# Expert tiles of two sizes: pairs of 128-slot units, and single units for an odd rest

## Chip, core and metric

The kernel runs on one core of one Trainium2 chip. The metric is the device time of that core in microseconds. Before the change it is 7677.54 us, the median of three runs (7675.36 to 7677.76).

## What is computed

The input is x, float32, 4 images of 256 channels by 64 x 64 pixels.

```
x = x + conv3(layernorm_over_channels(x))
t = tokens(x)                      # 4 x 4096 tokens of 256
z = layernorm(t)
probs = softmax(z @ gate_w + gate_b)          # 8 experts
for the two largest probs e of each token:
    t += probs[e] * (gelu(z @ W1[e] + b1[e]) @ W2[e] + b2[e])   # 256 -> 512 -> 256
x = pixels(t)
```

conv3 is three modulated deformable 3 x 3 convolutions in a row, each followed by relu. For every pixel and each of nine taps an offset and a mask are computed by an ordinary 3 x 3 convolution; the input is sampled bilinearly at the shifted place, scaled by the mask and multiplied by that tap's 256 x 256 weight. All of it is float32.

## The kernel before

**Convolutions.** An image is eight blocks of 512 pixels. A block of a layer is nine taps. For each tap and each 128 pixels, GpSimd gathers 128 rows of four corner vectors, 512 KB, from a table in HBM (`samples`, L503); VectorE combines them (L509, L514), ScalarE scales (L517), TensorE transposes (L532), ScalarE copies out of PSUM (L535), and TensorE multiplies with the tap's weight (`finish`, L555). That is four gathers a tap, 864 taps in the kernel, one after the other in the order of `self.stages`; the convolutions of one image and parts of the next alternate. `off_block` (L357 to L427) makes the offsets of a coming block.

**Experts.** When the last layer of a block is done, `tokens` makes its tokens, their normalised form and their two experts with weights. Tokens are taken in five groups: images 0, 1 and 2 whole (M = 32 columns of 128 tokens), image 3 in two halves (M = 16). When a group is complete, `route` (L690) gives each of its 2 x 128 x M token-expert pairs a slot, sorted by expert. An expert's slots begin at a multiple of 256 (FT), so that every tile of 256 slots belongs to one expert. A group has NF = 2 x M x 128 / 256 + 7 tiles, room enough whatever the routing: 39 for a whole image, 23 for a half; 163 in all, or 326 units of 128 slots. Tiles past the last used slot are worked like the others. `invert` (L768) turns slots into the list `tok` of the token in each slot by matmuls of one-hot matrices, and `wrow` holds the rows of the weight table for each tile. Where a tile's expert is that of the tile before in its chain, `wrow` points out of bounds and nothing is read.

A tile is worked by the generator `expert` (L825) in three pieces:
- `fetch` (L790), called at the end of the tile before, issues on GpSimd's queue the weights w (L800, 1.18 MB, two buffers in turn) and the token rows zt (L812, two gathers of 128 rows)
- piece 1: the y of the tile before is added and stored (`products`, L883: L892 and a store on SP's queue), four transposes (L840), one copy (L844)
- piece 2: 8 float32 matmuls of 256 columns, which stand in the trace as 16 records, two for each (L856), and four gelus (L866)
- piece 3: the next tile's fetch, then 8 matmuls of 256 columns, again 16 records (L874), into py

When all tiles of a group are done, `end` fetches each token's two results (L915), adds them with their weights (L930), transposes (L948) and stores.

**Order.** Tiles are taken from two chains in turn, f = 0, half, 1, half + 1, ... (`Group.order`), so that consecutive tiles use the two weight buffers. Pieces wait in three lanes (`Lane`): routes, tiles and sums. `pump` gives each lane one tap's credit after each tap of the convolution, and a lane runs pieces while its credit lasts. A tile costs `pace` taps: 5, 6, 2, 1.5 and 0 for the five groups. What is left after the last tap is drained: group 3 in part, group 4 entirely. `issue_after` keeps some instructions behind the newest gather, sum or transpose. A scheduler orders the instructions within these limits; each engine then works in its own order.

Of the kernel before, what the change touches and what calls it, by code (L numbers as in the profile page):

```python
# [8 lines left out]
F32 = mybir.dt.float32  # L9
# [73 lines left out]
class Group:  # L83


    def __init__(self, b, n0, n1):
# [4 lines left out]
        self.NF = 2 * self.M * P // FT + E - 1  # L91


        self.half = (self.NF + 1) // 2
        self.zt, self.acc, self.gy, self.sums, self.py = {}, [], [], [], None
        self.order = [s // 2 + s % 2 * self.half for s in range(self.NF)]

# [20 lines left out]
class Weave:  # L118
# [92 lines left out]
    def ffn_constants(self):  # L211
# [8 lines left out]
        nf = max(g.NF for g in self.groups)  # L220
        for g in self.groups:
            g.zd = self.dram.tile([g.M * P, C], F32, name=f"z_{g.nm}", tag=f"z_{g.nm}")
        self.ys = [
            self.dram.tile([nf * FT, C], F32, name=f"ys_{i}", tag=f"ys_{i}") for i in range(3)
# [42 lines left out]
        assert FU * nf <= P  # L267
# [422 lines left out]
    def route(self, grp):  # L690
# [3 lines left out]
        grp.tok = self.rt2.tile([P, FU * NF], I32, tag="tok", name=f"tok_{grp.nm}")  # L694
        grp.wrow = self.rt2.tile([P, NF], I32, tag="wrow", name=f"wrow_{grp.nm}")

        def small(tag, shape, dt=F32):
# [18 lines left out]
        nc.vector.tensor_scalar(ni, slot[:, :, M - 1], float(FT - 1), None, ALU.add)  # L716
        nc.vector.tensor_scalar(ni, ni, FT_LOG, None, ALU.logical_shift_right)
        nt = small("nt", (P, E))
        nc.vector.tensor_copy(nt, ni)
        end = small("end", (P, E))  # L720
        nc.vector.tensor_tensor_scan(end, self.ones[:, :E], nt, 0.0, ALU.mult, ALU.add)
        off = small("off", (P, E))
        nc.vector.tensor_tensor(off, end, nt, ALU.subtract)
        nc.vector.tensor_scalar(off, off, float(FT), None, ALU.mult)
        nc.vector.tensor_tensor(slot, slot, tot, ALU.subtract)
        nc.vector.tensor_tensor(slot, slot, rp[:, 0], ALU.add)
        nc.vector.tensor_tensor(
            slot, slot, off.unsqueeze(2).to_broadcast([P, E, M]), ALU.add
        )
        for i in range(2):  # L730
# [8 lines left out]
        past = small("r1", (P, NF, E))  # L739
        nc.vector.tensor_tensor(  # L740
            past,
            self.row_f[:, :NF].unsqueeze(2).to_broadcast([P, NF, E]),
            end.unsqueeze(1).to_broadcast([P, NF, E]),
            ALU.is_ge,
        )
        ex = small("ex", (P, NF))
        nc.vector.tensor_reduce(ex, past, AX.X, ALU.add)
# [18 lines left out]
        grp.inv = self.ps1.tile([P, FU * NF], F32, tag="py", name=f"inv_{grp.nm}")  # L766

    def invert(self, grp, m):  # L768
# [4 lines left out]
        n = FU * grp.NF  # L773
# [16 lines left out]
    def fetch(self, grp, step):  # L790
# [18 lines left out]
        for u in range(FU):  # L809
            zt = self.ffn.tile([P, C], F32, tag=f"zt{u}", name=f"zt_{grp.nm}_{f}_{u}")  # L810
            j = FU * f + u
# [13 lines left out]
    def expert(self, grp, step):  # L825
# [10 lines left out]
        zt = grp.zt.pop(step)  # L836
        tp = self.ps.tile([P, CC, FT], F32, tag="tp", name=f"ftp_{nm}")
        for u in range(FU):
            for c in range(CC):
                nc.tensor.transpose(  # L840
                    tp[:, c, u * P : (u + 1) * P], zt[u][:, c * P : (c + 1) * P], self.ident
                )
# [301 lines left out]
```

## Time and profile before

| | |
|---|---|
| median of three runs | 7677.54 us |
| the profiled execution | 6731.9 us, span 6730.2 us |
| granted TensorE clock in it | 0.979 |
| TensorE / VectorE / ScalarE / GpSimd busy | 92 / 74 / 49 / 66% of the span |
| bytes moved | 2228 MB, mean 331 GB/s |
| L503, gathers of the taps | 3456, 1059 ns each on GpSimd, 6.9 us to landing |
| L555, tap matmuls | 6912 records, 3404 us busy |
| L856, first expert matmul | 2608 records of 256 columns, 686 us busy |
| L874, second expert matmul | 2608 records of 256 columns, 659 us busy |
| L892, y | 163, 684 ns each |
| L800, weight fetches | 163 issued, 1112 ns each on GpSimd |
| L812, token gathers | 326, 1016 ns each on GpSimd |

The profiled execution is shorter than the runs of the median. Times below that come from the profile are those of this execution. PE is TensorE, PEld its weight loads, DVE VectorE, ACT ScalarE, POOL GpSimd, SP the sync engine that issues direct transfers. "L503" is line 503 of the kernel printed above. A group of instructions with one line is named by output and input tile, as in ph<-fzT,w. "Busy" of TensorE contains the pipelined ends of its matmuls, so the distance from one start to the next tells more than the duration of a record.

### The profile page before, as it was taken

The page shows a single profiled execution, that of the slowest core. Times are in us where ns is not written, and L with a number is a line of the kernel's source. Part 1 is how long each engine was busy: PE and PEld are TensorE (multiplying, and loading weights), DVE is VectorE, ACT ScalarE, POOL GpSimd, SP SyncE. Part 2 cuts the span into 40 slices and gives each one's busy share as a digit, 9 for nine tenths or more (in the row PEclk, how much of TensorE's full clock was granted, in tenths as well). Part 3 has the DMA queues.
Part 4 walks back from the last instruction along what each step waited for, and adds up shares of the span by engine and source line. Part 5 has one row for each costly group of instructions (what it writes and reads, how often), then busy time and mean ns, then how long its engine had stood idle before and what let it go on. Part 6 is the DMA issues. An engine that isn't in the chain of part 4 may idle for free. (4 is left out here: it accounts for less than half of the span.)

```text
span 6730.2 us, 88993 instructions
## 1 busy us (share of the span) xinstructions
PE 6193.9 (92%) x26500; PEld 3512.7 (52%) x26500; DVE 4955.9 (74%) x11467; ACT 3271.0 (49%) x7139; POOL 4463.9 (66%) x4245
## 2 busy tenths in 40 slices
PE   7999889899999999999999999999998999988987
PEld 3444344444555555555554555555554566655665
DVE  7878777899966767888977777667888764688511
ACT  3555555555544544555544554455554444444322
POOL 4656666666766666666777766666667775677643
PEclk9999999999999999999999999999999999999998
DMA  8999999999989989999899999989999997899744
GB/s 303 350 335 382 364 355 372 376 382 385 352 319 363 333 300 373 345 358 364 312 363 356 380 337 343 332 315 359 351 362 330 340 315 261 296 346 335 236 138 125
DMA packets 805215, 2228.45 MB, mean 331 GB/s; under 512 B 105016, under 2 KB 307768, under 8 KB 798976
## 3 DMA queue, kind: packets, MB, share of 16 engines
q0 software_dynamic: 551200, 1947.35, 78.3%
q1 hardware_dynamic: 253536, 275.41, 11.9%
q8 instruction: 215, 3.52, 0.2%
q14 instruction: 264, 2.16, 0.1%
HBM read 2165.40 MB, written 196.40 MB: 351 GB/s over the span
## 5 line engine op out<-in xcount | busy, mean ns | idle before, releaser
L503 POOL DMA_INDIRECT g<-tab,idx x3456 | 3660.1, 1059 | 1728.6 <-DVE s L514 602.0
L555 PE MATMUL acc<-sT,wk 128*128 128x512 f32 x6912 | 3404.2, 605 | 147.9 <-ACT sT L535 132.7
L509 DVE SCALAR_TENSOR_TENSOR g<-g,cf 128x512 f32<-128x512 f32 x3456 | 2558.2, 743 | 337.0 <-DMA g<-tab,idx 332.9
L514 DVE SCALAR_TENSOR_TENSOR s<-g,cf 128x256 f32<-128x256 f32 x3456 | 1658.4, 482 | 718.2 <-PE tp L532 438.3
L535 ACT COPY sT<-tp 128x512 f32<-128x512 f32 x1728 | 1001.5, 585 | 1852.9 <-PE tp L532 1850.3
L517 ACT ACTIVATE s<-s,cf 128x256 f32<-128x256 f32 x3456 | 1639.5, 508 | 360.0 <-DVE s L514 323.6
L555 PEld LDWEIGHTS acc<-sT,wk 128*128 128x128 f32 x6912 | 1161.3, 192 | 944.1 <-issue 641.3
L532 PEld LDWEIGHTS tp<-ident,s 128*128 128x128 f32 x6912 | 887.1, 143 | 1354.7 <-issue 661.7
L532 PE MATMUL tp<-ident,s 128*128 128x128 f32 x6912 | 1254.1, 280 | 185.6 <-ACT s L517 173.5
L856 PE MATMUL ph<-fzT,w 128*128 128x256 f32 x2608 | 686.3, 395 | 56.5 <-ACT fzT L844 31.9
L874 PE MATMUL py<-w,hT 128*128 128x256 f32 x2608 | 658.5, 387 | 28.8 <-ACT hT L866 25.4
L856 PEld LDWEIGHTS ph<-fzT,w 128*128 128x128 f32 x2608 | 479.9, 195 | 196.1 <-ACT fzT L844 67.7
L874 PEld LDWEIGHTS py<-w,hT 128*128 128x128 f32 x2608 | 469.1, 191 | 152.0 <-ACT hT L866 68.4
L866 ACT ACTIVATE hT<-ph,w 128x256 f32<-128x256 f32 x652 | 281.9, 471 | 462.3 <-PE ph L856 443.0
L812 POOL DMA_INDIRECT zt<-z,tok x326 | 331.3, 1016 | 152.0 <-issue 85.4
L357 PE MATMUL po<-win,wo 128*32 128x504 f32 (+1 forms) x2304 | 349.7, 597 | 1.0 <-ACT win L301 0.5
L915 POOL DMA_INDIRECT gy<-ys,slots x256 | 267.5, 1045 | 118.2 <-issue 73.2
L800 POOL DMA_INDIRECT w<-in_W,wrow x163 | 181.3, 1112 | 248.0 <-issue 122.3
L892 DVE TENSOR_TENSOR y<-py,w 128x512 f32<-128x512 f32 x163 | 111.5, 684 | 232.8 <-PE py L874 232.7
L930 DVE SCALAR_TENSOR_TENSOR ta<-gy,cw,ta 128x256 f32<-128x256 f32 x256 | 120.8, 480 | 109.3 <-DMA gy<-ys,slots 59.1
L357 PE MATMUL po<-win_pre,wo 128*32 128x504 f32 (+1 forms) x1152 | 187.1, 630 | 2.3 <-ACT om L366 2.0
L844 ACT COPY fzT<-ftp 128x512 f32<-128x512 f32 x163 | 95.4, 585 | 138.6 <-PE ftp L840 132.8
(154 smaller groups left out, 2902.5 us busy)
## 6 DMA issues: line engine op xcount, KB each, us to landing
tab<-hv SPq DMA_DIRECT2D x512, 128.0 KB
g<-tab,idx POOLq DMA_INDIRECT x3456, 6.9
ys<-y SPq DMA_DIRECT2D x163, 256.0 KB
tab<-h_pre SPq DMA_DIRECT2D x128, 256.0 KB
wk<-in_conv_w SPq DMA_DIRECT2D x117, 256.0 KB
xc_pre<-in_x SPq DMA_DIRECT2D x32, 512.0 KB
xr_tok<-in_x SPq DMA_DIRECT2D x32, 512.0 KB
t<-t_tok SPq DMA_DIRECT2D x32, 512.0 KB
```

What stands on the lines that cost most here:

```text
L357: nc.tensor.matmul(po[g * Q : (g + 1) * Q, :].rearrange("q (r w) -> q r w", w=W)[:, :, x0:x1], lhsT=self.wo[l][:, 3 * ky + kx, c, :], rhs= ...
L503: self.gathered = nc.gpsimd.indirect_dma_start(out=g.rearrange("p x s f -> p (x s f)"), out_offset=None, in_=self.table(*self.stages[i][:2 ...
L509: nc.vector.scalar_tensor_tensor(g[:, :, 0, :], g[:, :, 1, :], cf[:, j, 0:1], g[:, :, 0, :], ALU.mult, ALU.add,)
L514: self.last = nc.vector.scalar_tensor_tensor(s, g[:, 1, 0, :], cf[:, j, 1:2], g[:, 0, 0, :], ALU.mult, ALU.add)
L517: nc.scalar.activation(s, s, AF.Copy, scale=cf[:, j, 2:3])
L532: self.turned = nc.tensor.transpose(tp[:, c, u * P : (u + 1) * P], ss[u][:, c * P : (c + 1) * P], self.ident)
L535: nc.scalar.copy(self.sT[:, :, t0 * P : (t0 + 2) * P], tp)
L555: nc.tensor.matmul(acc[:, o, :], lhsT=self.wk[k][:, c, o * P : (o + 1) * P], rhs=sT[:, c, :], start=(k == 0 and c == 0), stop=(k == K - 1 ...
L812: self.nc.gpsimd.indirect_dma_start(out=zt, out_offset=None, in_=grp.zd, in_offset=bass.IndirectOffsetOnAxis(ap=grp.tok[:, j : j + 1], axi ...
L856: nc.tensor.matmul(ph[:, h, :], lhsT=w1[:, o : o + P], rhs=zT[:, c, :], start=(c == 0), stop=(c == CC - 1),)
L866: nc.scalar.activation(ht[:, h, :], ph[:, h, :], AF.Gelu, bias=w1[:, k : k + 1])
L874: nc.tensor.matmul(py[:, u, :], lhsT=hT[h // 2][:, h % 2, u * P : (u + 1) * P], rhs=w2[:, h * C : (h + 1) * C], start=(h == 0), stop=(h == ...
```

## The change

An expert with u units of 128 slots now gets u // 2 tiles of two units and, where u is odd, one tile of one unit. A group then needs at most 2 x M + 7 units: 71 in place of 78 for an image, 39 in place of 46 for a half. The first NP tiles (31 or 15) are pairs, the last nine are singles, 40 or 24 tiles in all. Pairs of all experts come first, in the order of experts, then the odd units in the order of experts; pairs beyond NP are worked as two singles.

`route` computes the slots from two running counts, one of pairs and one of odd units, and the expert of each tile likewise. A single transposes, multiplies, adds and stores half as much; its weight fetch is whole. The pace of a single is half that of a pair. `half` and the two chains are formed as before, from the new number of tiles.

```diff
-        self.NF = 2 * self.M * P // FT + E - 1
+        self.NU = 2 * self.M + E - 1
+        self.NP = (self.NU - E - 1) // FU
+        self.NF = self.NP + E + 1
...
+    def units(self, f):
+        return (FU * f, FU) if f < self.NP else (f + self.NP, 1)
...
-        nc.vector.tensor_scalar(ni, slot[:, :, M - 1], float(FT - 1), None, ALU.add)
-        nc.vector.tensor_scalar(ni, ni, FT_LOG, None, ALU.logical_shift_right)
+        nc.vector.tensor_scalar(ni, slot[:, :, M - 1], float(P - 1), None, ALU.add)
+        two = small("two", (P, 2, E), I32)
+        nc.vector.tensor_scalar(two[:, 0], ni, FT_LOG, None, ALU.logical_shift_right)
+        nc.vector.tensor_scalar(
+            two[:, 1], ni, FT_LOG - 1, 1, ALU.logical_shift_right, ALU.bitwise_and
+        )
...
+        over = small("r1", (P, E, M))
+        nc.vector.tensor_tensor(over, slot, cut.unsqueeze(2).to_broadcast(every), ALU.is_ge)
         nc.vector.tensor_tensor(
-            slot, slot, off.unsqueeze(2).to_broadcast([P, E, M]), ALU.add
+            over, over, off[:, 1].unsqueeze(2).to_broadcast(every), ALU.mult
+        )
+        nc.vector.tensor_tensor(slot, slot, over, ALU.add)
+        nc.vector.tensor_tensor(
+            slot, slot, off[:, 0].unsqueeze(2).to_broadcast(every), ALU.add
         )
...
+        for v in range(2):
+            past = small("r1", (P, NF, E))
+            nc.vector.tensor_tensor(
+                past,
+                first.unsqueeze(2).to_broadcast([P, NF, E]),
+                end[:, v].unsqueeze(1).to_broadcast([P, NF, E]),
+                ALU.is_ge,
+            )
+            nc.vector.tensor_reduce(part if v else ex, past, AX.X, ALU.add)
...
-        for u in range(FU):
+        q, fu = grp.units(f)
+        for u in range(fu):
             zt = self.ffn.tile([P, C], F32, tag=f"zt{u}", name=f"zt_{grp.nm}_{f}_{u}")
-            j = FU * f + u
+            j = q + u
...
-        nc.scalar.copy(zT, tp)
+        nc.scalar.copy(zT[:, :, :n], tp[:, :, :n])
...
                     nc.tensor.matmul(
-                        ph[:, h, :],
+                        ph[:, h, :n],
                         lhsT=w1[:, o : o + P],
-                        rhs=zT[:, c, :],
+                        rhs=zT[:, c, :n],
...
-                nc.scalar.activation(ht[:, h, :], ph[:, h, :], AF.Gelu, bias=w1[:, k : k + 1])
+                nc.scalar.activation(
+                    ht[:, h, :n], ph[:, h, :n], AF.Gelu, bias=w1[:, k : k + 1]
+                )
...
-        for u in range(FU):
+        for u in range(fu):
             for h in range(HC):
                 nc.tensor.matmul(
                     py[:, u, :],
...
-            self.ys[grp.i % 3][f * FT : (f + 1) * FT, :].rearrange("(u p) c -> p u c", u=FU),
-            y,
+            self.ys[grp.i % 3][q * P : (q + fu) * P, :].rearrange("(u p) c -> p u c", u=fu),
+            y[:, :fu],
...
             gen = self.expert(grp, step)
+            pace = grp.pace * grp.units(grp.order[step])[1] / FU
             for _ in range(3 + (step == 0)):
-                self.tiles.put(grp.pace / 3, lambda gen=gen: next(gen, None))
+                self.tiles.put(pace / 3, lambda gen=gen: next(gen, None))
```

## The prediction, made before the change was timed

> **What bounds the kernel now.** I read the page's first part, then the busy time of each engine in five stretches, then the tap gathers in the same stretches, then TensorE's timeline.
>
> ```profile
> PE 6193.9 (92%) x26500; PEld 3512.7 (52%) x26500; DVE 4955.9 (74%) x11467; ACT 3271.0 (49%) x7139; POOL 4463.9 (66%) x4245
> ...
> DMA packets 805215, 2228.45 MB, mean 331 GB/s; under 512 B 105016, under 2 KB 307768, under 8 KB 798976
> ...
> q8 instruction: 215, 3.52, 0.2%
> q14 instruction: 264, 2.16, 0.1%
> ```
>
> TensorE is far ahead of the other engines, but a busy share of pipelined matmuls overstates, so the stretches decide (columns: stretch, length, busy us of PE, PEld, DVE, ACT, POOL, granted clock, DMA share, GB/s). The first has no expert tiles, the next three have those of images 0, 1 and 2 beside the taps, the last is the drain.
>
> ```profile
> 672.00:1176.00 504.00, 448.56 (x1758) 204.96 (x1758) 390.34 (x772) 254.16 (x562) 338.07 (x322) 1.00 0.96 364
> 1848.00:3024.00 1176.00, 1119.29 (x4798) 637.62 (x4796) 864.53 (x1890) 603.10 (x1327) 772.36 (x746) 0.99 0.93 342
> 3528.00:4872.00 1344.00, 1251.55 (x5235) 692.75 (x5235) 987.52 (x2010) 678.31 (x1487) 931.74 (x890) 0.99 0.94 347
> 5208.00:5880.00 672.00, 654.77 (x2938) 422.91 (x2937) 421.51 (x859) 316.18 (x695) 448.74 (x440) 1.00 0.87 303
> 6384.00:6680.00 296.00, 265.34 (x1177) 214.08 (x1177) 46.74 (x110) 69.52 (x160) 108.92 (x112) 0.94 0.41 126
> ```
>
> Without tiles the DMA share is 0.96 and TensorE has 11% free; beside tiles TensorE is at 93 to 97% and the DMA share falls. So taps alone are bound by the gathers, taps with tiles by TensorE, with the DMA close behind; the drain by TensorE and its waits. How far each holds is read from the gathers of L503 (POOL's count) in the same stretches:
>
> ```profile
> 672.00:1176.00 504.00, 338.07 (x322) 1.00 0.96 364
> 1848.00:3024.00 1176.00, 670.06 (x649) 0.99 0.93 342
> 3528.00:4872.00 1344.00, 799.66 (x768) 0.99 0.94 347
> 5208.00:5880.00 672.00, 296.84 (x290) 1.00 0.87 303
> ```
>
> A gather takes 504/322 = 1.565 us without tiles. The 649 of image 0's stretch would then take 1016 us; the other 160 us fell to about 33 tiles (counted by the y adds of L892), 4.9 us a tile. The same sum gives 142/32 = 4.4 us for image 1 and 218/34 = 6.4 us for image 2. TensorE's own time for a tile follows from its timeline, start to start:
>
> ```profile
> 3000.86 1.04 PE L532 MATMUL tp<-ident,s 128*128 128x128 f32 x8
> 3001.96 1.99 PE L856 MATMUL ph<-fzT,w 128*128 128x256 f32 x8
> 3003.79 3.60 PE L555 MATMUL acc<-sT,wk 128*128 128x512 f32 x8
> 3007.22 3.62 PE L874 MATMUL py<-w,hT 128*128 128x256 f32 x16
> 3010.67 1.04 PE L532 MATMUL tp<-ident,s 128*128 128x128 f32 x8
> ```
>
> Sixteen py records take 3.45 us, 216 ns each; eight acc records of 512 columns 3.43 us, 429 ns each; transposes of 128 columns 110 ns. Time is by columns. A tile has 16 ph and 16 py records and 4 transposes: 3.45 + 3.45 + 0.44 = 7.35 us. So a tile costs the stretch 0.6 to 0.9 of its TensorE time, because the taps alone would have waited for gathers anyway. In the drain it costs more than that time:
>
> ```profile
> 6659.41 2.86 PE L874 MATMUL py<-w,hT 128*128 128x256 f32 x12 [0.19 <-ACT hT L866]
> ...
> 6667.61 2.86 PE L874 MATMUL py<-w,hT 128*128 128x256 f32 x12 [0.19 <-ACT hT L866]
> ```
>
> One tile each 8.20 us, with 0.56 and 0.19 us of waits for gelu, and longer waits where new weights come.
>
> [...] the 16 lp_tok matmuls of 8 columns took 1.71 us, 107 ns each[...]. [...] the weight fetch of 1.18 MB here landed in a median of 5.9 us:
>
> ```profile
> DMA to landing us min/median/max: 3.3/5.9/10.4
> ```
>
> **The change, part by part.** Each group loses 8 tiles of two units and gains 9 of one (39 to 31 + 9, in the halves 23 to 15 + 9).
>
> TensorE: a single has 16 ph records of 128 columns, 8 py records and 2 transposes. The ph record isn't in the trace: between 107 ns (load and stream overlapped) and 214 ns (one after the other). I take 110, as the transposes, which load a new operand each time too, run so; the other end is a rival. That makes 1.76 + 1.73 + 0.22 = 3.71 us. A group saves 8 x 7.35 - 9 x 3.71 = 25.4 us, or 3.46 tiles; the five save 127 us of TensorE. On the path: image 0 3.46 x 4.9 = 17, image 1 15, image 2 22, and the two halves of image 3, whose tiles lie mostly in the drain, 3.46 x 8.2 = 28 each. Sum 110 us.
>
> Weights: the expert of each tile follows from the routed pairs. Running the reference's router on its inputs gives 9 9 8 8 9 8 9 9 units in group 0 (the others alike: 3 to 5 odd experts a group), which makes 45 real fetches before and 13, 12, 12, 13, 12 = 62 after, as each odd expert's single needs its weights again. The page confirms the 45: packets of 8 KB or more are 805215 - 798976 = 6239, less 215 + 264 of instructions = 5760 = 45 x 128 rows. Bytes: 17 x 1.18 = +20 MB, less 35 units x 262 KB of zt and y = -9 MB. In images 0 to 2 that is 10 fetches less 21 units, +6.3 MB, 18 us at 345 GB/s; these stretches are bound by DMA for about 0.4 of a tile, so 7 us. Bounds 0 and 31 us.
>
> Weight waits: two buffers take turns, so a fetch starts when the tile before the current one has been added (L892) and has the current tile to hide behind. It takes 1.0 us of POOL and 5.9 of DMA, 6.9 us, against 8.2 us for a pair and some 4.1 us for a single. In the drain, pairs alternate with singles; the last group refetches for four pairs after a single, at 2.8 us each 11 us, and for one after a pair, some 3 us, where the drain now shows five waits of 0.8 to 3.1 us (9 us) beside a first one of 8.5. I take +5 us, and +5 for the half before it. Beside taps a single spans 3 to 0.75 taps, a tap being four gathers, 6.3 to 9.3 us; from the add to the next ph are two to three pieces more, so I count nothing there; if the cover goes, it is the rival below. POOL's fetch stands before gathers in its queue; before the drain it never waited for the add.
>
> DVE: 18 more operations in each route: three of 256 elements (nearest rows 360 ns), a compare and a reduction of 320 (420 ns each), 13 small ones of about 200 ns, 4.5 us. Beside taps DVE is 74% busy and hides it; the last group's route stands in the drain, so 5 us. Bounds 0 and 22. ACT, POOL and SP: 20 gelus, 5 copies more, 35 zt gathers less, 5 fetches and 5 stores more, under 15 us of engines with half or a third of their time free: nothing. A single keeps its gelu hops (0.75 us) for half the work: 5 more tiles, 4 us. In the changed program's order the scheduler puts tap or other transposes into most of these gaps.
>
> Sum in the profiled execution: 110 - 7 - 10 - 5 - 4 = 84 us less of 6731.9 (span 6730.2), so 6648. The runs shown have a median of 7677.54, 1.14 times that, for a reason that no view shows. If all stretches, the saving is 96 us. If the time is TensorE at a lower clock, all tap stretches become TensorE-bound: my count of its streams is some 5740 us of the 6730[...]. Three runs within 2.4 us of each other look more like an engine than like contended DMA, so I lean to the second: 117 us, 7560.
>
> **The rivals.**
> Load-bound ph: records at 214 ns add 45 x 16 x 0.104 = 75 us, at 0.75 on the path 56; 84 - 56 = 28, 7645. Against it: loads hide wholly behind 216 ns records. For it: nothing here streams 128 columns against a plain float32 load.
> DMA-bound timed runs: images 0 to 2 give nothing and pay 18 us; 56 - 18 - 19 = 19 us, 7655. For it: DMA shares of 0.93; against: TensorE is busier in the same stretches.
> Slower: the weight wait shows at every single, beside taps as well, since POOL waits in order for the buffer and holds the tap gathers behind it. Price 2.8 us at the single and 2.8 at the pair after it, 45 x 5.6 = 252 us in place of my 10; it decides from about 2 us a single (94/45). Then 84 + 10 - 252, 158 us more, by 1.14 is 180: 7858. For it: image 2's singles pass in one tap; against: a tap there is 9 us, above 6.9.
>
> **How the numbers follow.** Forecast 0.69, load-bound 0.10, DMA-bound 0.12, slower 0.09. About 0.2% (15 us) is what a measurement can tell from no change. The two middle cases lie at its edge, half of each within: faster 0.69 + 0.06 + 0.06 = 0.81, same 0.10, slower 0.09. The forecast's own range is 7500[...] to 7620; with the middle cases 7500 to 7655.
>
> **What would show it.** PE records: ph 1968 of 256 columns and 720 of 128, py 2328; a 128-column ph stream at 110 ns start to start; 5760 + 17 x 128 = 7936 large packets of weights; the stretches of images 0 to 2 ending some 15 to 20 us earlier each; single after single in the drain about 4 us apart and a wait for w before pairs that change expert. It is wrong if TensorE idles on w beside taps, if POOL's gathers wait at L892, or if ph records stand 200 ns apart.

## The result, and the profile after

The changed kernel takes 7719.55 us (median of four runs, 7702.26 to 7728.05) against 7676.45 us for the kernel before on the same chip: a ratio of 1.0052, 95% interval 1.0037 to 1.0067. It is slower by about 40 us, where 117 us less was forecast. The runs come from six sessions, each with its own runs of the kernel before; in five of them that kernel took 7572 to 7696 us, in the last 6738, so ratios are formed within a session only, and what compares two sessions says so. The five sessions of the experiments were on five chips, and the last chip is the fast one: whether its speed is the chip's own or comes from something else, no run tells. The profile shown of before, at 6731.9 us, is none of the runs whose median stands beside it. Below, the last session is the faster one, the others are the slower ones.

The page of the changed kernel (time 7702.26 us, span 7700.6, clock 0.932):

```profile
PE 6367.4 (83%) x26230; PEld 3539.4 (46%) x26230; DVE 4940.9 (64%) x11562; ACT 3248.5 (42%) x7156; POOL 4474.5 (58%) x4215
...
DMA packets 799855, 2239.33 MB, mean 291 GB/s; under 512 B 103081, under 2 KB 301353, under 8 KB 791441
...
q8 instruction: 213, 3.49, 0.2%
q14 instruction: 266, 2.17, 0.1%
```

The counts are those forecast: 270 records less on TensorE (26500 to 26230), and 799855 - 791441 - 213 - 266 = 7935 large packets, 62 weight loads. But TensorE is busy for 83% of the span, not for 92%: in this execution it waits for 1333 us. A profile of the kernel before in a slower session (run e0 below, span 7531.4) is the right neighbour:

```profile
PE 6413.4 (85%) x26500; PEld 3600.9 (48%) x26500; DVE 4940.0 (66%) x11467; ACT 3268.0 (43%) x7139; POOL 4480.1 (59%) x4245
```

Four of its stretches, each from the sum of one tap to that of another (taps counted from 0), and the drain: taps 72 to 252 (no tiles), 360 to 468 (image 0's last tiles), 576 to 720 (image 1's last), 756 to 863 (image 2's). Columns as in the prediction:

```profile
628.00:1854.00 1226.00, 1073.89 (x4283) 528.75 (x4282) 980.32 (x2337) 599.66 (x1312) 791.88 (x718) 0.96 0.94 346
...
2708.00:3612.00 904.00, 811.30 (x3478) 467.50 (x3477) 655.90 (x1686) 430.44 (x930) 531.33 (x492) 0.95 0.86 307
...
4500.00:5616.00 1116.00, 965.48 (x3879) 529.89 (x3879) 760.55 (x1628) 520.81 (x1127) 675.79 (x646) 0.97 0.87 310
...
5943.00:7091.00 1148.00, 959.43 (x3953) 608.70 (x3952) 647.05 (x1440) 455.14 (x990) 646.41 (x633) 0.94 0.76 262
7091.00:7531.00 440.00, 349.93 (x1549) 277.41 (x1547) 101.20 (x275) 101.55 (x226) 188.37 (x193) 0.90 0.43 134
```

The same taps in the changed kernel:

```profile
633.00:1868.00 1235.00, 1071.83 (x4282) 525.48 (x4281) 981.70 (x2352) 600.38 (x1312) 783.36 (x720) 0.96 0.94 345
...
2730.00:3714.00 984.00, 802.35 (x3443) 457.96 (x3442) 666.29 (x1721) 427.49 (x936) 550.49 (x507) 0.91 0.81 290
...
4590.00:5768.00 1178.00, 968.69 (x3831) 524.67 (x3830) 767.59 (x1651) 515.05 (x1130) 701.69 (x662) 0.93 0.85 301
...
6099.00:7271.00 1172.00, 950.77 (x3900) 600.82 (x3900) 636.88 (x1442) 447.48 (x990) 637.47 (x613) 0.92 0.72 252
7271.00:7700.00 429.00, 313.54 (x1414) 240.53 (x1412) 97.33 (x286) 94.12 (x230) 170.03 (x175) 0.85 0.45 147
```

TensorE is busy 9 us less at taps 360 to 468 and 756 to 863, 3 more at 576 to 720, and 36 less in the drain. The time does not follow: taps 360 to 468, where image 0's singles stand, take 80 us more (taps without tiles 9 more, so the sessions differ by under 1% there); taps 576 to 720, with image 1's, take 62 more, taps 756 to 863 take 24 more, and the drain is 11 us shorter. At taps 360 to 468 TensorE is busy for 82% and the share of the DMA falls to 0.81, against 87% and 0.94 at the taps without tiles, so engines wait. One such wait is plain on POOL. Weight fetches at taps 418 to 435, the kernel before (e0) first, start and length, and in brackets the idle time before:

```profile
3189.58 1.03 POOL L800 DMA_INDIRECT w<-in_W,wrow  x1 [0.30 <-issue]
3235.70 1.01 POOL L800 DMA_INDIRECT w<-in_W,wrow  x1 [0.30 <-issue]
3279.15 1.04 POOL L800 DMA_INDIRECT w<-in_W,wrow  x1 [0.30 <-issue]
```

The changed kernel:

```profile
3231.55 1.34 POOL L838 DMA_INDIRECT w<-in_W,wrow  x1 [0.31 <-issue]
3262.77 1.00 POOL L838 DMA_INDIRECT w<-in_W,wrow  x1 [9.95 <-DVE g L513]
3302.93 1.03 POOL L838 DMA_INDIRECT w<-in_W,wrow  x1 [0.30 <-issue]
3340.76 1.41 POOL L838 DMA_INDIRECT w<-in_W,wrow  x1 [3.71 <-ACT win_pre L471]
3378.64 1.00 POOL L838 DMA_INDIRECT w<-in_W,wrow  x1 [0.30 <-issue]
3404.64 1.00 POOL L838 DMA_INDIRECT w<-in_W,wrow  x1 [9.08 <-ACT s L521]
```

Before every second fetch POOL now stands, that is, it idles with the gathers queued behind it, for up to 16.7 us. The fetch is the one that a single's step issues for the tile after it: the single's pace is half, so the last reader of the buffer is half as far behind (this reason is argued). Between taps 378 and 440 POOL stands for 70.5 us before fetches, 4.0 in e0. The experiments ask whether this is the price.

### The profile page after: what moved, and what is told of

Read it like the earlier page. It is cut to its first block, busy times and chain, and to the rows that moved or that the text cites. A ratio compares the mean times of both kernels' runs of the same rounds, so it can differ in the third digit from the quotient of the medians.

```text
span 7700.6 us, 88494 instructions
## 1 busy us (share of the span) xinstructions
PE 6367.4 (83%) x26230; PEld 3539.4 (46%) x26230; DVE 4940.9 (64%) x11562; ACT 3248.5 (42%) x7156; POOL 4474.5 (58%) x4215
## 2 busy tenths in 40 slices
DMA packets 799855, 2239.33 MB, mean 291 GB/s; under 512 B 103081, under 2 KB 301353, under 8 KB 791441
## 4 chain that ended last, share of the span: by engine, by line
PE 66%; ACT 10%; issue 9%; another core or an unknown queue 8%; DVE 4%; DMA 2%; POOL 1%; SPq 0%; ACTq 0%; POOLq 0%; DVEq 0%
PE acc L559 33%; PE tp L536 10%; PE ph L897 6%; PE py L917 6%; PE po L361 6%; ACT sT L539 3%; ACT s L521 3%; DVE g L513 1%; PE pm L375 1%; DVE s L518 1%; ACT hT L907 1%; PE lp_tok L622 1%; DMA w<-in_W,wrow 1%; PE tpv L329 1%
## 5 line engine op out<-in xcount | busy, mean ns | idle before, releaser
L507 POOL DMA_INDIRECT g<-tab,idx x3456 | 3710.6, 1074 | 2367.1 <-DVE s L518 1085.9
L559 PE MATMUL acc<-sT,wk 128*128 128x512 f32 x6912 | 3527.1, 625 | 303.2 <-ACT sT L539 153.3
L536 PE MATMUL tp<-ident,s 128*128 128x128 f32 x6912 | 1298.9, 287 | 588.9 <-ACT s L521 320.5
L559 PEld LDWEIGHTS acc<-sT,wk 128*128 128x128 f32 x6912 | 1207.4, 199 | 1171.5 <-issue 879.5
L897 PE MATMUL ph<-fzT,w 128*128 128x256 f32 (+1 forms) x2688 | 659.5, 382 | 149.8 <-issue 41.1
L907 ACT ACTIVATE hT<-ph,w 128x256 f32<-128x256 f32 (+1 forms) x672 | 271.6, 445 | 648.1 <-PE ph L897 359.7
L917 PEld LDWEIGHTS py<-w,hT 128*128 128x128 f32 x2328 | 433.4, 200 | 226.4 <-ACT hT L907 90.1
L936 DVE TENSOR_TENSOR y<-py,w 128x512 f32<-128x512 f32 (+1 forms) x168 | 103.3, 615 | 471.3 <-PE py L917 406.0
L851 POOL DMA_INDIRECT zt<-z,tok x291 | 292.2, 1004 | 156.7 <-issue 81.0
L885 ACT COPY fzT<-ftp 128x512 f32<-128x512 f32 (+1 forms) x168 | 89.0, 530 | 215.6 <-PE ftp L881 116.5
```

Source lines behind the costliest of these rows:

```text
L507: self.gathered = nc.gpsimd.indirect_dma_start(out=g.rearrange("p x s f -> p (x s f)"), out_offset=None, in_=self.table(*self.stages[i][:2 ...
L536: self.turned = nc.tensor.transpose(tp[:, c, u * P : (u + 1) * P], ss[u][:, c * P : (c + 1) * P], self.ident)
L559: nc.tensor.matmul(acc[:, o, :], lhsT=self.wk[k][:, c, o * P : (o + 1) * P], rhs=sT[:, c, :], start=(k == 0 and c == 0), stop=(k == K - 1 ...
L851: self.nc.gpsimd.indirect_dma_start(out=zt, out_offset=None, in_=grp.zd, in_offset=bass.IndirectOffsetOnAxis(ap=grp.tok[:, j : j + 1], axi ...
L897: nc.tensor.matmul(ph[:, h, :n], lhsT=w1[:, o : o + P], rhs=zT[:, c, :n], start=(c == 0), stop=(c == CC - 1),)
L907: nc.scalar.activation(ht[:, h, :n], ph[:, h, :n], AF.Gelu, bias=w1[:, k : k + 1])
```

## The experiments

The expectations name theories by letters. A: the stalls belong to the condition of the timed runs, in both kernels; B: they come with the change. In e1 and e3, C is that a single's pieces follow each other too closely, D that singles cost by their number, E that the loss is the weights loaded again. From e4 on, C is that a tile costs by its columns on TensorE, and F that it costs by its number, through its hand-offs between TensorE and ScalarE. G (POOL's wait at the fetch), H, I, K and L came as these fell. The price of an edit to the changed kernel is its ratio less 1.0052, times the time of the kernel before in its session; it carries about +-20 us and compares two sessions, so two chips.

**e0. The kernel before, again.** No edit.

> The kernel before, unchanged, for a profile under the conditions of the timed runs: the profile that the prediction read spans 6730 us with a clock of 0.979, the timed runs are at 7676, and the profile of the changed kernel spans 7701 at 0.932. Theory A (the timed condition is one in which TensorE itself stalls now and then, in both kernels): a span near 7675, a clock near 0.93, TensorE idle about 1300 us in place of 530, with many gaps of 3 us and more. Theory B (the stalls come with the change alone): a span near 6730 and fewer than 20 such gaps. Ratio to the kernel before 1.000.

Ratio 1.000 (0.9988 to 1.0013). So A holds: most stalls belong to the slower sessions, in both kernels. TensorE's waits for the scaled sums, in e0:

```profile
PE tp L532 <- ACT s L517: 284.9, 242, 13.8
```

and in the profile shown of before, where no such wait passes 2.6 us:

```profile
PE tp L532 <- ACT s L517: 173.5, 249, 2.6
```

ScalarE, which scales these sums, waits longer too. Its copy of the transposed sums and the idle time before it, in the profile shown of before, in e0 and in the changed kernel:

```profile
L535 ACT COPY sT<-tp 128x512 f32<-128x512 f32 x1728 | 1001.5, 585 | 1852.9 <-PE tp L532 1850.3
...
L535 ACT COPY sT<-tp 128x512 f32<-128x512 f32 x1728 | 1002.7, 585 | 2331.5 <-PE tp L532 1502.6 <-remote 422.4 <-issue 272.8
...
L539 ACT COPY sT<-tp 128x512 f32<-128x512 f32 x1728 | 1005.5, 587 | 2417.2 <-PE tp L536 1556.5 <-remote 484.7 <-issue 277.5
```

"Remote" and "issue" mark waits whose end no instruction of the program explains. Summed over all of ScalarE's instructions from tap 72 on they are 1179 us in e0, 1390 in the changed kernel, and 6 in the profile shown of before. At taps 360 to 468 they are 123 us in e0 and 231 in the changed kernel, the 80 us of that stretch and more. What causes them, and how much of the time they cost, the traces do not tell, and no run tested it.

**e1. One pace for all tiles, unscaled.**

```diff
-            pace = grp.pace * grp.units(grp.order[step])[1] / FU
+            pace = grp.pace
```

> The changed kernel, but every tile, single or pair, costs the full pace of its group, so that a single's three pieces stand as far apart among the taps as a pair's did. Theory C (a single's pieces follow each other too fast in images 0 to 2, and TensorE waits for the copy, the gelus and the weights): most of the loss goes, 7600 to 7660. Theory D (the singles cost by their number: fetches, hops, and their share in the drain): no gain, 7700 to 7760, or more since more tiles are left for the drain.

1.0043 (1.0020 to 1.0065). Taps 360 to 468 fall to 903 us, and POOL no longer stands there; but taps 468 to 576 take 37 us and taps 756 to 863 take 57 us more than in e0; 40 tiles at a full pace take 13 taps more over the three images. ScalarE's unexplained waits at taps 360 to 468 fall with the stretch, to 101 us. The place of the loss moves, the sum hardly.

**e2. The kernel before with fewer tiles**: 37 (20 for a half image), the 12 pairs that these inputs leave empty left out.

```diff
-        self.NF = 2 * self.M * P // FT + E - 1
+        self.NF = 37 if self.M == 32 else 20
```

> The kernel before with 37 and 20 tiles of two units in place of 39 and 23: the tiles left out hold no pair for these inputs, so 24 units go and no single comes. If a unit removed is worth what the prediction took from the profile (84 us for 35 units, scaled by 1.14 for the timed runs), 24 units give 24/35 x 110 x 1.14 = 86 us: 7590. If in the timed condition an expert tile beside taps costs nothing because TensorE waits for something else anyway, only the two halves' tiles count, 6 x 8.2 = 49 us: 7627. If it gives near nothing, the expert work is no part of the bound at all.

0.9870 (0.9851 to 0.9889): 93 us less by the medians, 7.7 us a pair. A whole tile is worth about what the prediction took for one (its prices give 81 us for these 12, 92 scaled by 1.14). Its columns are not what makes it worth that, as e4 to e6 show.

**e3. Singles load no weights** (they use those in the buffer; the fetch instructions stay).

```diff
+        nc.vector.memset(same[:, grp.NP :], 1.0)
```

> The changed kernel without the weight fetches of the singles: a single uses the weights that lie in its buffer, those of another expert, so the odd units are computed with wrong weights; 21 fetches of 1.18 MB go. Theory E (the 17 additional fetches and the waits for them are the loss): 7570 to 7640. Theory C or D: within 20 us of the changed kernel, 7700 to 7720.

1.0040 (1.0020 to 1.0061), with 41 loads in place of 62: 9 +- 20 us less. The bytes of these loads are at most a small part of the price.

**e4. Without the 12 singles that stay empty.**

```diff
-        self.NU = 2 * self.M + E - 1
+        self.NU = 2 * self.M + 5 if self.M == 32 else 36
```

> The changed kernel without the 12 singles (2 of an image's 9, 3 of a half image's) that these inputs leave empty. Theory F (a tile costs by its number, about 7.8 us each whatever its width, because it has as many hand-offs between TensorE and ScalarE): 12 x 7.8 = 94 us less than the changed kernel, so 0.993 of the kernel before. Rival C (a tile costs by its columns on TensorE, a single 3.7 us beside taps and 4.6 us after the last tap): 12 x 3.7 to 4.6 = 45 to 55 us less, 0.998 to 0.999 of the kernel before.

0.9952 (0.9930 to 0.9975): 77 +- 21 us less, 6.4 us a single, nearer F's 7.8 than the 4 of its columns. These 12 come last in their groups, and over half of the gain is in the drain (387 us against 430).

**e5. Four pairs a group worked as eight singles.** A scratch tile is made smaller to fit.

```diff
-        self.NP = (self.NU - E - 1) // FU
+        self.NP = (self.NU - E - 1) // FU - 4
```

> The changed kernel with 4 pairs a group split into 8 singles: 20 tiles more, and the same 71 or 39 units. The columns on TensorE stay the same. Theory F: 20 x 7.8 = 156 us more than the changed kernel, 1.026 of the kernel before. Rival C: the columns are the same, so 0 to 20 us more, 1.005 to 1.008.

1.0206 (1.0177 to 1.0234): 118 +- 25 us more for 20 tiles more with the same columns (four more loads among them), 5.9 us each, between the two forecasts and far nearer F's. POOL's fetches in the changed kernel, with busy time and the idle time before them:

```profile
L838 POOL DMA_INDIRECT w<-in_W,wrow x168 | 189.0, 1125 | 581.8 <-issue 170.8
```

and in e5:

```profile
L838 POOL DMA_INDIRECT w<-in_W,wrow x188 | 211.3, 1124 | 667.1 <-issue 229.3 <-ACT s L521 131.3 <-ACT sT L539 77.0
```

POOL's time at the fetches grows by 108 us, near the 118. That suggested G; that the two are the same time isn't shown by it.

**e6. Singles stream 256 columns in the first product** (each column twice).

```diff
-                        ph[:, h, :n],
+                        ph[:, h, :],
...
-                        rhs=zT[:, c, :n],
+                        rhs=zT[:, c, :n] if fu == FU else zT[:, c, :P].unsqueeze(1).to_broadcast([P, FU, P]),
```

> The changed kernel whose singles stream 256 columns through the first product (the 128 twice) in place of 128; the gelu and all else stay at 128. 45 singles x 16 matmuls x 0.111 us = 80 us more of TensorE time, and no hand-off more. Theory F: the columns lie in TensorE's idle time, 0 to 20 us more than the changed kernel, 1.005 to 1.008 of the kernel before. Rival C: 60 to 80 us more, 1.013 to 1.016.

1.0072 (1.0045 to 1.0099): 15 +- 24 us more, for 80 us of columns by count. Its page has 91 us more of TensorE than the changed kernel's (busy time also moves by itself: e7 and e10, with the changed kernel's columns, have 38 and 112 us more):

```profile
PE 6458.2 (83%) x26230; PEld 3606.2 (47%) x26230; DVE 4946.6 (64%) x11562; ACT 3242.1 (42%) x7156; POOL 4480.9 (58%) x4215
```

So in a slower session TensorE's columns cost about a fifth of their time, and by the interval at most half.

**e7. One gelu hand-off for a single in place of two**: all four chunks in one PSUM tile of the same size.

```diff
-        for h0 in range(0, HC, 2):
-            ph = self.ps1.tile([P, 2, FT], F32, tag="ph", name=f"ph_{nm}_{h0}")
+        for h0 in range(0, HC, two):        # two = 4 for a single, 2 for a pair
+            ph = self.ps1.tile([P, two, n], F32, tag="ph", name=f"ph_{nm}_{h0}")
```

> The changed kernel whose singles compute all four chunks of the hidden layer into one PSUM tile of the same size, so that a single has one hand-off to the gelu in place of two. TensorE's and ScalarE's instructions are the same in number and shape. Theory F: a single has three hand-offs in place of four, a quarter of 7.8 us x 45 = 88 us less at most, half of that if the second pass is half hidden: 0.994 to 1.000 of the kernel before. Rival C: nothing changes, 1.005 +- 0.002.

1.0059 (1.0037 to 1.0082): 5 +- 21 us more, where a hand-off less was to give up to 44 or 88 us. A hand-off is not 2 us; F's mechanism falls, though its count of tiles stands.

**e8. Singles issue no weight fetch** (they use the weights in the buffer).

```diff
+        if step < 2 or f < grp.NP:
             self.nc.gpsimd.indirect_dma_start(
                 out=self.w[step % 2][:, : W1N + W2N],
```

> The changed kernel whose 45 singles issue no weight fetch (they compute with the weights of the tile two steps before them in the order, so the output is not the reference's); 5 groups x 9 instructions fewer on POOL, everything else as in the changed kernel. Theory G (a tile costs by its weight fetch: POOL waits in order for the buffer's last readers, and the taps' gathers stand behind it; 3.5 us of wait and 1.1 us of issue each in the changed kernel's profile): 45 x 4.6 = 207 us less at most, half of it if the gathers catch up: 0.978 to 0.992 of the kernel before. Theory F (a tile costs by its hand-offs between TensorE and ScalarE): 0 to 20 us less, 1.002 to 1.005.

1.0005 (0.9988 to 1.0022): 36 +- 17 us less for 45 fetches, 21 of which load, 0.8 us each. But these are issued in the step ahead, mostly a pair's; the fetches that stand are those issued in a single's step, and they stayed.

**e9. Only the first two fetches of a group**, whose weights all its tiles use: the same edit with `if step < 2:`.

> The changed kernel with only the first two weight fetches of a group (all other tiles compute with those two experts' weights, so the output is not the reference's): 165 instructions fewer on POOL and 52 loads of weights fewer. Theory G: 165 x 4.6 = 760 us less at most; the 200 or so tiles then cost at least their issue elsewhere, so 300 to 700 us less, 0.91 to 0.965 of the kernel before. Theory F: only the loads' share of the queues and the waits for weights after the last tap, 0 to 60 us less, 0.997 to 1.005.

0.9647 (0.9628 to 0.9666): 311 +- 19 us less for 158 instructions, 52 of which load (the expectation's 165 was a slip: 168 less two for each of five groups), 2.0 us each, whichever tile's step issues the fetch. The fetch is a third of a tile's price. Taps 360 to 468 fall from 984 to 894 us, below e0's 904, so the loss there goes when all these fetches go.

**e10. The fetch a piece later** beside taps, at the start of the step that uses it, behind the y add of the step before.

```diff
+        if grp.has < step:
+            with self.after(self.gathered):
+                self.weights(grp, step)
```

> The changed kernel with the weight fetch of a step beside taps issued a piece later (at the start of the step that uses it, after the y add of the step before, in place of with the third piece of the step before), the gathers of its tokens where they were. The buffer's last reader is then a full step behind in place of two thirds. Theory G: POOL's idle time before the fetches falls from about 580 us by a half or more and the time by 50 to 200 us, 0.98 to 0.999 of the kernel before, unless the weights then come late to TensorE. Theory F: no change or slower by the weights that come late, 1.005 to 1.02.

1.0040 (1.0024 to 1.0055): 9 +- 17 us less. POOL now stands at most 0.7 us before a fetch of images 0 and 1, yet taps 360 to 468 still take 965 us. The stand on POOL is a sign, not the price.

**e11. The y add reads the tokens**, so VectorE does not wait for TensorE there.

```diff
-                py[:, :fu],
+                py[0].unsqueeze(1).to_broadcast([P, fu, C]),       # py is now the list of zt
```

> The changed kernel whose y add takes the tile's gathered tokens in place of the second product (the output is not the reference's): all instructions stay, but VectorE, which works in order and has the taps' sums queued behind the y add, no longer waits for TensorE there. Theory I (a tile costs by the places where VectorE, ScalarE and POOL, which run ahead of TensorE, stand still for TensorE, and so lose their lead): the 470 us of idle time before the y adds go, 100 to 350 us less than the changed kernel, 0.96 to 0.99 of the kernel before. Rival H (only TensorE's own queue matters, VectorE catches up by its idle third): 0 to 30 us less, 1.001 to 1.005.

1.0071 (1.0045 to 1.0096): no gain. VectorE's idle time before L936 falls from 471 to 199 us, and this is worth nothing.

**e12. Singles do nothing on TensorE and ScalarE**; fetch, gather, y add (of the tokens) and store stay.

```diff
+        if fu == 1:
+            yield
+            ...
+            grp.py = (f, zt[0].unsqueeze(1), w2)
+            return
```

> The changed kernel whose 45 singles do nothing on TensorE and ScalarE: weight fetch, token gather, y add (of the tokens) and store stay (the output is not the reference's). A single cost about 6 us in the runs with fewer and more of them, 0.8 us of it by its fetch. Theory I: its three waits on TensorE are gone, 45 x 4 to 5 us = 180 to 225 us less than the changed kernel, 0.975 to 0.982 of the kernel before. Rival H: only its TensorE time counts, of which the run with doubled columns showed a fifth on the path, 45 x 0.5 to 1 us = 20 to 45 us less, 0.999 to 1.003.

0.9995 (0.9983 to 1.0008): 43 +- 15 us less, 1 us for all of a single's 3.7 us of TensorE (by the prediction's count), its copy and its four gelus. Taps 360 to 468 still take 970 us.

**e14 and e15. Eight pieces a tile**, each waiting ScalarE or VectorE instruction a piece behind the TensorE work that it waits for, handed out every half tap; in the changed kernel and in the kernel before.

```diff
+        yield
         nc.scalar.copy(zT[:, :, :n], tp[:, :, :n])
...
+            yield
             ht = self.ffn.tile([P, 2, FT], F32, tag="hT", bufs=3, name=f"hT_{nm}_{h0}")
...
-            for _ in range(3 + (step == 0)):
-                self.tiles.put(pace / 3, lambda gen=gen: next(gen, None))
+            for _ in range(8 + (step == 0)):
+                self.tiles.put(pace / 8, lambda gen=gen: next(gen, None))
```

> The changed kernel with a tile's work cut into eight pieces in place of three, so that each ScalarE or VectorE instruction that waits for TensorE stands a piece later in its queue than the TensorE work that it waits for, and pieces handed out every half tap. All instructions stay. Theory I: 50 to 200 us less than the changed kernel, 0.978 to 0.998 of the kernel before. Rival H: no change within 0.3%, 1.002 to 1.008.

> The kernel before with the same eight pieces and half taps. Theory I: 40 to 190 us less than the kernel before, 0.975 to 0.995; and as the waits are then hidden, the changed kernel with eight pieces is not slower than this one. Rival H: no change within 0.3%, and the changed kernel with eight pieces 0.5% slower than this one.

1.0084 (1.0061 to 1.0107) and 1.0081 (1.0060 to 1.0102). Theory I (a tile costs by the places where the other engines wait for TensorE) falls: nothing is gained by the spacing, and the kernel before loses 0.8%. With eight pieces the two kernels are level.

The last three ran in the session in which the kernel before takes 6737.8 us.

**e16. No fetch in a single's step**: the tile after a single uses the weights that are there.

```diff
+        if step < 2 or grp.units(grp.order[step - 1])[1] == FU:
             self.nc.gpsimd.indirect_dma_start(
```

> The changed kernel without the weight fetches that a single's step issues for the tile after it (that tile, mostly a pair, computes with the weights of the tile two steps before it, so the output is not the reference's). In the traces POOL idles 0.3 us before a fetch beside the taps of images 0 and 1 in the kernel before, and 8 to 17 us before each one that a single's step issues in the changed kernel, because the half pace halves the distance to the buffer's last reader. Theory K (this stall is what the change lost): 0.985 to 0.995 of the kernel before. Rival L (more steps for the same taps, whatever their fetch: TensorE, ScalarE and VectorE have 16 tiles to hand on where they had 12): 1.000 to 1.006.

0.9873 (0.9859 to 0.9888): 86 us less than the kernel before. 40 fetches are gone, 14 of them loads, so 48 loads are left against the 45 of before.

**e17. The changed kernel on the taps of the kernel before.**

```diff
-            pace = grp.pace * grp.units(grp.order[step])[1] / FU
+            pace = grp.pace * (grp.M + 7) / grp.NF
```

> The changed kernel with all tiles, single or pair, handed out at one pace, and that scaled by 39/40 (23/24 for the half images), so that a group's tiles take the taps that they take in the kernel before: 195, 234 and 78. In the run with the pace by tile, unscaled, taps 360 to 468 took 903 us against 984 in the changed kernel and 904 in the kernel before, but the lane was 13 taps longer in all and the last image's taps took 57 us more. Theory K and L both: without the squeeze and without the longer lane the singles' smaller work shows: 0.990 to 1.000 of the kernel before. Rival F (a tile costs by its number): 5 tiles more, 35 units less, 1.004 to 1.006 as the changed kernel.

0.9993 (0.9985 to 1.0002): no difference, though TensorE is busy 6116.7 us against 6193.9.

**e18. The kernel before, squeezed**: nine of its pairs at half the taps, where the changed kernel has singles.

```diff
+            pace = grp.pace / (1 if grp.order[step] < grp.NF - 9 else 2)
```

> The kernel before, with 9 of an image's tiles handed out at half the taps, in the places where the changed kernel has its singles; they stay pairs, and no work is added or removed. Theory K and L: the squeeze alone costs, most of it at taps 360 to 468 and 576 to 720: 1.008 to 1.020 of the kernel before. Rival F: nothing is added, 0.998 to 1.003.

1.0008 (1.0002 to 1.0015). POOL's standing before fetches beside taps rises from 141 to 239 us, and 6 us is all that it costs. K (the standing is what the change lost) falls with it, in the faster session at least.

**Where e17's saved TensorE time went.** The kernel before at taps 360 to 468, 468 to 576, 756 to 863 and in the drain:

```profile
2486.00:3292.00 806.00, 777.48 (x3482) 453.26 (x3481) 656.53 (x1686) 429.97 (x930) 529.54 (x496) 0.99 0.94 347
3292.00:4060.00 768.00, 709.52 (x2975) 388.44 (x2974) 572.60 (x1165) 383.44 (x836) 573.81 (x540) 0.98 0.96 354
...
5341.00:6302.00 961.00, 908.52 (x3942) 589.38 (x3941) 651.06 (x1438) 459.31 (x989) 655.52 (x632) 0.99 0.88 312
6302.00:6730.00 428.00, 344.89 (x1531) 271.92 (x1529) 101.60 (x276) 99.28 (x220) 188.38 (x193) 0.89 0.46 141
```

e17:

```profile
2498.00:3284.00 786.00, 745.25 (x3399) 428.36 (x3398) 656.66 (x1700) 427.71 (x934) 517.75 (x483) 1.00 0.94 352
3284.00:4071.00 787.00, 720.49 (x2987) 389.31 (x2986) 573.45 (x1168) 383.65 (x837) 584.28 (x548) 0.98 0.95 349
...
5359.00:6314.00 955.00, 891.31 (x3901) 571.85 (x3900) 650.82 (x1462) 453.63 (x999) 654.05 (x625) 0.98 0.87 314
6314.00:6733.00 419.00, 309.71 (x1418) 238.39 (x1416) 98.91 (x288) 92.82 (x228) 176.55 (x181) 0.86 0.48 155
```

From tap 72 to the last tap TensorE is busy 43 us less, and the time is 5733 us against 5726: what the first of these stretches gains the second gives back, at DMA shares of 0.94 to 0.96, where taps alone have 0.97. In the drain TensorE is busy 35 us less, and 9 arrive. The same stretch in e16:

```profile
6281.00:6646.00 365.00, 294.88 (x1407) 232.70 (x1405) 97.97 (x286) 91.04 (x225) 156.20 (x160) 0.89 0.47 151
```

A pair that changes its expert behind a single, in e17's drain:

```profile
6542.16 1.13 PE L917 MATMUL py<-w,hT 128*128 128x256 f32 x4
6543.13 0.71 PE L881 MATMUL ftp<-ident,zt 128*128 128x128 f32 x5
6546.83 3.19 PE L897 MATMUL ph<-fzT,w 128*128 128x256 f32 x8 [2.99 <-DMA w<-in_W,wrow]
6550.59 1.22 PE L917 MATMUL py<-w,hT 128*128 128x256 f32 x2 [0.57 <-ACT hT L907]
6551.60 3.22 PE L897 MATMUL ph<-fzT,w 128*128 128x256 f32 x8
```

and a pair behind a single in e16's, where nothing is fetched:

```profile
6491.08 1.13 PE L918 MATMUL py<-w,hT 128*128 128x256 f32 x4
6492.05 1.89 PE L898 MATMUL ph<-fzT,w 128*128 128x256 f32 x8
6493.78 0.71 PE L882 MATMUL ftp<-ident,zt 128*128 128x128 f32 x5
6494.51 0.70 PE L918 MATMUL py<-w,hT 128*128 128x256 f32 x2
6495.04 1.89 PE L898 MATMUL ph<-fzT,w 128*128 128x256 f32 x8
```

The wait of 2.99 us is not the whole price: after it the same eight records take 3.19 and 3.22 us in place of 1.89, at a lower granted clock (1.00 from 6540 to 6546, 0.65 from 6546 to 6551, 0.67 from 6551 to 6556). Nor is this one an exception. In the profile shown of before, a wait of 8.48 us for weights is followed by two passes of eight ph records in 3.78 and 3.62 us, at a granted clock of 0.50 from 6474 to 6484. And 28 of TensorE's 41 pauses of over 1.5 us there are followed by records that stand, in the median of the next eight, at least 1.5 times their usual distance apart (some of these pauses come close behind another). Not all are: behind one of 2.32 us, before 6506, the granted clock is 1.00 up to 6512. e16's drain is 365 us against e17's 419: 54 us of their difference of 85. The wait for weights in the drain, in us, times and longest, in the kernel before:

```profile
PE ph L856 <- DMA w<-in_W,wrow: 22.8, 7, 8.5
```

in e17:

```profile
PE ph L897 <- DMA w<-in_W,wrow: 40.4, 13, 5.7
```

and in e16:

```profile
PE ph L898 <- DMA w<-in_W,wrow: 10.4, 4, 4.0
```

## Why the prediction was wrong, step by step

- **The price of columns: the step that failed.** The prediction took what a stretch pays for a tile (4.9, 4.4, 6.4 us, in the drain 8.2), divided it by the tile's TensorE time, and multiplied it with the TensorE time saved: "On the path: image 0 3.46 x 4.9 = 17, image 1 15, image 2 22", and 28 for each half. A tile's price is real (7.7 us in e2, 6.4 in e4), but it does not go by columns: 80 us more of them cost 15 +- 24 (e6), the same columns in 20 more tiles cost 118 (e5), and all of a single's work on TensorE and ScalarE is worth 1 us (e12). These are slower sessions; in the faster one e17 got 7 us more beside taps in place of 54 less, and in the drain 9 less in place of 56.
- **TensorE's own sum was nearly right for the tiles, and too large for the engine.** The short ph records did not turn out load-bound. In the changed kernel:

```profile
3269.00 1.16 PE L897 MATMUL ph<-fzT,w 128*128 128x128 f32 x8 [1.82 <-issue]
3269.99 0.60 PE L536 MATMUL tp<-ident,s 128*128 128x128 f32 x4
```

  Eight records take 0.99 us: the first, behind a pause, stands 214 ns ahead of the second, and the others 111 to 112 ns apart, where 110 was assumed and the rival had 214 for all. (The 3.45 us for a pair's ph is a little low: eight records take 1.83 us in the prediction's own lines, so sixteen some 3.66.) The 62 loads and the 720 short and 1968 long ph and 2328 py records were as counted. The groups of the tiles (ph, py, ftp) are busy 119 us less in e17 than in the kernel before, and 105 less in the changed kernel than in e0, near the 127. But TensorE in all is busy only 77 and 46 us less, because other groups grew: the tap transposes and offsets by 24 us in e17, the tap matmuls by 33 us in the changed kernel (625 ns a record against 619).
- **Weights, +7 us for loads and +10 for waits.** The bytes are about right (e3: 9 +- 20). That TensorE waits for weights in the drain alone was right as well, and the waits themselves were nearly so: 28 us in the changed kernel against 16 in e0, 40 in e17 against 23 in the kernel before. What the term lacked is that in e17's drain the waits of 3 to 5.7 us are followed by one or two slow passes of eight records, 1.3 to 1.9 us more each (those behind the wait of 2.99 at a granted clock of 0.65 and 0.67), and the price of the fetch instruction. e17 and e16 differ by 85 us, 2.1 us for each of 40 fetches, of which the drain has 54. With e8's 0.8 us a single would cost 2.7 us in fetches (0.8 + 85/45, an estimate over two kinds of session), beyond the "about 2 us a single" from which the slower rival was to decide, at half that rival's price. Three limits: e16 keeps the single's half pace and e17 doesn't (e18 puts that at 6 us); e16 also lacks 26 fetches that load nothing; and 2.1 us is what e9 gives for a fetch in any step, so the kernel before would be expected to gain as well from leaving out 40 of its own, which was not run.
- **The slower rival's mechanism.** POOL's in-order wait behind singles is in the trace, as it said. As a cost beside taps it isn't borne out: e10 takes the standing away and e18 adds 98 us of it, both with next to no effect. The time moved the way this rival said, but not by its mechanism, as far as the runs show.
- **VectorE's route, gelu hops (5 and 4 us).** No run isolates VectorE's; in e7, 45 hops less gave no gain (5 +- 21 us more).
- **Timed runs as scaled profile: wrong.** The prediction leaned to TensorE being the bound at a lower clock, and scaled the gain up. How low that clock would be was the author's assumption, which no run shows, and that runs within 2.4 us of each other speak for an engine was a guess: the 117 us, and the 7500 at the lower end of the range, rest on them, where the profile's own sum, scaled by 1.14, gives 96. e0 shows the opposite: TensorE at 85%, its waits longer, with a granted clock of 0.946 over the run; the 5740 us of streams stand without their working. Columns are worth little there (15 +- 24 us for 80, e6).

What is settled: the tiles' TensorE time was saved, 105 to 119 us of it, and did not shorten the run, in either kind of session. In the faster one e16 suggests where it went: with the fetches behind singles gone, 86 us appear; with them, nothing. In the drain this is in the trace, as waits and slow passes; for the rest, and for the missing run of before with fewer fetches, it is argued. What stays open: the loss in the slower sessions. By the prices above (an estimate) 40 pairs less at 7.7 us save 308 us and 45 singles at 5.9 to 6.4 cost 266 to 288, so the change would gain 20 to 42 us, and it lost 40. The loss shows at the singles of images 0 and 1 and moves when the pace is changed (e1). Loads (9 +- 20, e3) and POOL's standing (9 +- 17, e10) don't carry it; all of the singles' work on TensorE and ScalarE (43 +- 15, e12) is as large, but stands in place of more work in the pairs, and without it taps 360 to 468 stay long. There ScalarE's waits without a releaser in the program grow, and these exist in the slower sessions alone; whether they are cause or company no run tested. A tile's 6 us are explained to a half: 2.0 by the fetch, 1 by TensorE and ScalarE. The changed kernel itself was not run in the faster session, nor e16 in the slower. Keeping the right weights while sparing those fetches, for example with a third weight buffer, was not tried. Of the versions that compute the reference only e2 and e4 beat the kernel before, and their tile counts fit these inputs alone.

## What to carry to other kernels

A stage's price for a unit of work may not be scaled by one of its parts: change that part alone (double its columns) before trusting it. Smaller tiles keep every fixed step (a fetch alone 2.0 us in e9), and shorten the time behind which the next tile's fetch can hide (here 5.9 us to landing, behind 8.2 us of a pair in the drain), so count the fetches per microsecond of work, not per kernel. Before forecasting for timed runs from a profile that is 12% shorter, look for what the two differ in, and whether they ran on the same chip; here the difference was mostly waits (TensorE's 1118 us in place of 536), many of them ended by nothing in the program.

## What the runs showed of the hardware

The same kernel took 6738 us on one chip and 7572 to 7696 us in sessions on others. In the two profiles, with a granted TensorE clock of 0.979 and 0.946, TensorE is busy only 3.5% more in the long one (6413 against 6194 us) and waits for 1118 us in place of 536: 182 waits of over 1.5 us with 638 us in all, against 42 with 127. Single waits for the scaled sums reach 13.8 us against 2.6, and ScalarE's waits without a releaser in the program make 1179 us against 6. In e17's drain the records behind each of four waits of 3 to 5.7 us for weights took another 1.5 to 4 us; behind the wait of 2.99 us the granted clock was 0.65 to 0.67, and behind one of 8.48 us in the profile shown of before 0.50. No weight fetch of the changed kernel takes POOL less than 0.99 us, though for 106 of the 168 nothing is read.
